# Group-norm statistics of the later batches through a DRAM round trip instead of two matrix products, in an attention kernel on one core

## The chip, the core and the metric

The kernel runs on one NeuronCore of a Trainium2 chip. The metric is the device time in microseconds (us) of one execution. Five engines work side by side, each through its own instructions in order: TensorE (PE in the profile, its weight loads PEld), VectorE (DVE), ScalarE (ACT), GpSimd (POOL) and SyncE (SP, here a queue for DMAs). They meet through semaphores.

## What is computed

The reference takes x of 32 images x 256 channels x 32 x 32 positions in float32, normalises it in groups of 8 channels, runs masked attention with 8 heads of 32 channels over the 1024 positions, and adds the result to x:

```python
def _gn(v, G=32, eps=1e-5):
    g = v.reshape(B_, G, C_ // G, H_, W_)
    m = jnp.mean(g, axis=(2, 3, 4), keepdims=True)
    s = jnp.var(g, axis=(2, 3, 4), keepdims=True)
    return ((g - m) / jnp.sqrt(s + eps)).reshape(v.shape)
# attention on _gn(x)
q = einsum('oc,bcs->bos', q_w, xf) + q_b     # likewise k and v from kv_w, kv_b
scores = einsum('bhqd,bhkd->bhqk', q, k) / sqrt(dk)
attn = softmax(where(mask == 0, -10000.0, scores)) with masked entries 0
out = einsum('bhqk,bhkd->bhqd', attn, v)
x = x + out
```

The mask keeps keys strictly before the query.

## The kernel before, in words

The function `unshifted` holds the whole fast path; `shifted` is a fallback that runs only when sums leave a range. Channels lie on the 128 partitions, in two halves g (NG = 2). A batch is one image. Its attention is cut into 12 visits: 6 per half g, each one entry of VISITS (line 583) with a long and a short block of scores for four heads. The loop over i at the end of `unshifted` runs 384 visits plus one. In each turn it emits `scores` of visit i, what is due `at` i, `values` of visit i - 1, what is due `between`, `add_keys` of visit i - 1, and what is due `after`. All five engines keep the order in which the code emits (`manual_schedule`, line 660), so these lists are an order written out by hand.

`scores(b, v)` (line 348) makes three PSUM tiles sT: two for the long block (heads 0 and 1, heads 2 and 3), one for the short block. The pool ps_s holds three such tiles, so each visit overwrites those of the visit before. In turn come the short products of heads 2 and 3, the long ones of heads 0 and 1, the long ones of heads 2 and 3, a wait of TensorE for the semaphore bank_free, and the short products of heads 0 and 1. Where a visit has two long entries and is in PAIRS (line 592), the second long entry of heads 0 and 1 is put between the two short products of heads 2 and 3, whose order is then turned round. A product is written by line L311 of the profile. ScalarE then takes the exponentials of the two long tiles (L397, written to e) and of the short one (L393, written to eh). For visits in PAIRS GpSimd masks eh into a diagonal tile with two selects (L339).

`values` (line 412) multiplies the exponentials with v into acc (L422). `add_keys` (line 434) sums exponentials on VectorE for the softmax denominators (L440): after visit 3's values comes one sum of 2048 elements per partition, after visit 4's first the sum e + diagonal, then e + e. `fold` and `stack` (lines 449 and 455) bring those sums together across partitions, by accumulating DMAs from GpSimd's queue and by SyncE's DMAs into folded; `finish` (line 539) multiplies, adds bias and residual on VectorE (L544, L547) and stores through SyncE.

One projection of the next batch (q, k or v, L169, from the normalised xn) is emitted in each visit, so the statistics of batch b are made while batch b - 1 is in its visits. `prepare(b, whens)` (line 637) lays them out with PREPARE (line 652), counted in visits from the first visit of b:

- `norm_channels`, once per half: two bn_stats (L184) and one bn_aggr (L185) on VectorE give each channel's mean and variance in mv.
- `norm_mean`: TensorE multiplies the means with avg (four products into pm, L169), ScalarE negates the result (L195).
- `norm_deviation`: three small VectorE instructions (L205 to L207).
- `norm_variance`: four products into pv, ScalarE adds eps (L219).
- `norm_rstd` (line 221): GpSimd raises to the power -0.5 (L227), then multiplies mean and rstd to shift (L229).
- `norm_apply` (line 231): ScalarE writes xn (L244). The first application stands in the after-list of the batch's visit 5, ahead of visit 6's exponentials on ScalarE.

For batches 2 to 31, pm comes after visit 3's scores and the values of visit 2, pv one visit later. Batch 0 is prepared ahead of the loop with its own forms of these steps, batch 1 in the first visits of batch 0. ALIGN (line 658) puts 24 drains on VectorE and 64 waits on GpSimd at the start.

Of the kernel before, what the change touches and what calls it, by code (L numbers as in the profile page):

```python
# [9 lines left out]
F32 = mybir.dt.float32  # L10
I32 = mybir.dt.int32
AF = mybir.ActivationFunctionType
ALU = mybir.AluOpType
# [4 lines left out]
P = 128  # L18
HD = 32
CPG = 8  # L20
HALF = 512
# [11 lines left out]
def tile_norm_attention_residual(  # L33
# [19 lines left out]
    nc = tc.nc  # L53
    B, C, H, W = x.shape
    S = H * W
    NG = C // P
    NB = S // P
    NH = S // HALF
# [3 lines left out]
    const = ctx.enter_context(tc.tile_pool(name="const", bufs=1))  # L62
# [26 lines left out]
    in_range = const.tile([P, ROW], F32, name="in_range")  # L89
    nc.gpsimd.memset(in_range, 1.0)  # L90
    inv_last = const.tile([P, 4, HALF // HD], F32, name="inv_last")
    eps = const.tile([P, 1], F32, name="eps")
    nc.gpsimd.memset(eps, 1e-5)

# [4 lines left out]
    def unshifted():  # L99
        live = {}  # L100
# [78 lines left out]
        def norm_channels(b, g):  # L179
            if g == 0:  # L180
                live["mv", b] = small.tile([P, NG, 2], F32, tag="mv", name=f"mv_{b}")
            st = small.tile([P, NH, 6], F32, tag="st", name=f"st_{b}_{g}")
            for c in range(NH):
                nc.vector.bn_stats(st[:, c, :], live["x", b][:, g, c * HALF : (c + 1) * HALF])  # L184
            nc.vector.bn_aggr(live["mv", b][:, g, :], st)  # L185

        def norm_mean(b):
            mv = live["mv", b]
            pm = misc(f"pm_{b}")
            product(pm[:, :NG], avg, mv[:, :, 0])  # L190
            if b == 0:
                live["dev", b] = small.tile([P, NG], F32, tag="dev", name=f"dev_{b}")
                nc.vector.tensor_sub(live["dev", b], mv[:, :, 0], pm[:, :NG])
            mean = small.tile([P, NG], F32, tag="mean", name=f"mean_{b}")
            nc.scalar.activation(mean, pm[:, :NG], AF.Identity, scale=-1.0)  # L195
            live["minus_mean", b] = mean

        def norm_deviation(b):
            mv, minus_mean = live["mv", b], live["minus_mean", b]

            if b == 0:
                dev = live["dev", b]
            else:
                dev = small.tile([P, NG], F32, tag="dev", name=f"dev_{b}")
                nc.vector.tensor_add(dev, mv[:, :, 0], minus_mean)  # L205
            nc.vector.tensor_mul(dev, dev, dev)
            nc.vector.tensor_add(dev, dev, mv[:, :, 1])  # L207
            live["dev", b] = dev

        def norm_variance(b):  # L210
            pv = misc(f"pv_{b}")
            product(pv[:, :NG], avg, live.pop(("dev", b)))
            rstd = small.tile([P, NG], F32, tag="rstd", name=f"rstd_{b}")
            live["rstd", b] = rstd
            if b == 0:

                nc.vector.tensor_scalar_add(rstd, pv[:, :NG], 1e-5)
                return
            nc.scalar.activation(rstd, pv[:, :NG], AF.Identity, bias=eps)  # L219

        def norm_rstd(b):
            rstd = live["rstd", b]
            if b == 0:

                nc.gpsimd.tensor_tensor(rstd, rstd, power, ALU.pow)
                return
            nc.gpsimd.tensor_tensor(rstd, rstd, power, ALU.pow)  # L227
            live["shift", b] = small.tile([P, NG], F32, tag="shift", name=f"shift_{b}")
            nc.gpsimd.tensor_tensor(live["shift", b], live["minus_mean", b], rstd, ALU.mult)  # L229

# [76 lines left out]
        def score(b, g, bank, j, op):  # L307

            c, kb, first, width, cols = op
            rows = slice(HD * j, HD * (j + 1))  # L310
            return nc.tensor.matmul(  # L311
                bank[c : c + KEYS, cols], lhsT=live["k", b, g][rows, kb * P + c : kb * P + c + KEYS],
                rhs=live["q", b, g][rows, first : first + width], start=True, stop=True, skip_group_check=True,
            )

        def scores_of(b, g, bank_of, heads, entries, between=lambda: None, order=slice(None)):
# [9 lines left out]
                                done.setdefault((j, c), []).append(score(b, g, bank_of(j), j, ops[n]))  # L326
            return done

        def mask(b, g, raw, j):


            hf, place = j // 2, (2 * j % 4) * P
            if ("e", b, g, "D", hf) not in live:
                live["e", b, g, "D", hf] = epool.tile(
                    [P, 4, HALF], F32, tag=("e0", "e")[hf], bufs=4, name=f"diagonal_{b}_{g}_{hf}"
                )
            square = live["e", b, g, "D", hf]
            for s in range(2):
                nc.gpsimd.affine_select(  # L339
                    out=square[:, :, place + s * P : place + (s + 1) * P],  # L340
                    in_=raw[:, :, (1 - s) * KEYS : (3 - s) * KEYS],
                    pattern=[[0, 4], [(1, -1)[s], P]], compare_op=ALU.is_gt, fill=0.0, base=0,
                    channel_multiplier=(-1, 1)[s],
                )
            if j == 0:
                nc.gpsimd.memset(square[0:1, :, 0:1], 1.0)

        def scores(b, v):
# [12 lines left out]
            long_of = lambda heads, n: scores_of(b, g, lambda j: pairs[j // 2][:, j % 2, :], heads, longs[n : n + 1])  # L361
            rest = [lambda: long_of((2, 3), 1)] if len(longs) > 1 else []
            begin = [lambda n=n: long_of((0, 1), n) for n in range(len(longs) - 1, -1, -1)]
            if i in PAIRS and len(longs) > 1:
                first = short_of((2, 3), begin.pop(0), slice(None, None, -1))
            else:
                first = short_of((2, 3))
# [222 lines left out]
        ]  # L590
        N, TOTAL = NG * len(VISITS), 2
        PAIRS = {0: 0, 1: 1, 3: 3, 4: 2}

        PRODUCTS = [
            (0, [
# [33 lines left out]
            10: [(("L", 4, Q(0, 4)), Q(0, 4)), (("D", 1, Q(0, 4)), Q(0, 4))],  # L629
            11: [(("L", 5, Q(0, 3)), Q(1, 4)), (("L", 5, Q(3, 4)), Q(3, 4)), (("H", 5, Q(0, 2)), Q(2, 4))],  # L630
        }
        at, between, after = {}, {}, {}

        def when(i, f, where=at):
            where.setdefault(i, []).append(f)

        def prepare(b, whens):
            for n, f in zip(whens, [
                lambda: norm_channels(b, 0), lambda: norm_channels(b, 1), lambda: norm_mean(b),
                lambda: norm_deviation(b), lambda: norm_variance(b), lambda: norm_rstd(b),  # L640
            ] + [lambda hf=hf, g=g: norm_apply(b, hf, g) for hf in range(NH) for g in range(NG)]):
                if n is None:
                    f()
                elif isinstance(n, tuple):
                    when(n[0], f, between)
                else:
                    when(n, f, after)

        PROJECT = (-5, -4, -3, -2, -1, 0, 1, 2, 3, 4, 5, 6)
        PREPARE = (-12, -11, -9, -9, -8, -8, -7, -6, -5, -3)
        SUMS = (3, 7, 10, 13)
        LOAD = 7
        SPREAD = (2, 2, 4, 5)
        FINISH = (N + 13, N + 13, N + 14, N + 16)
        every = range(4)
        ALIGN = 24, 64

        with tc.manual_schedule(engines={ENG.PE, ENG.Activation, ENG.DVE, ENG.Pool, ENG.SP}):  # L660

# [20 lines left out]
            if B > 1:  # L682
                nc.scalar.sem_inc(live["arrived"], 1)
                nc.sync.wait_ge(live["arrived"], 2)
                load(1)
            norm_deviation(0)
            norm_variance(0)
            turn_weights(0)
# [13 lines left out]
                else:  # L702
                    when(n, f)
            if B > 1:
                prepare(1, (None, None, 0, 1, 2, 2, 3, 4, 5, 7))
            for b in range(B):
                first, last = b * N, b == B - 1
                if b >= 1:
# [2 lines left out]
                if b >= 2:  # L711
                    for n in range(NG * NH):
                        cols = slice(n % NH * HALF, (n % NH + 1) * HALF)
                        v = max(first - 2 * N + LOAD, 0)
                        if n % NH == 0:
                            when(v, lambda n=n: with_scores(n // NH))
                        when(v, lambda b=b, n=n, cols=cols: load_part(b, n // NH, cols))
                    prepare(b, [(first + n,) if k in (2, 3) else first + n for k, n in enumerate(PREPARE)])
                if not last:
                    for n in every:  # L720
                        v = first + SUMS[n]
# [28 lines left out]
            for i in range(B * N + 1):  # L750
                if i < B * N:
                    scores(*divmod(i, N))
                for f in at.pop(i, ()):
                    f()
                b, v = divmod(i - 1, N)
                if i == B * N:

                    sums(3, SUMMED[v], False)
                if i:
                    values(b, v)  # L760
                    for f in between.pop(i, ()):
                        f()
# [7 lines left out]
            assert not at and not between and not after  # L770
            inside = end_last(B - 1)
        for p in reversed(pools):
            p.release()
# [171 lines left out]
```

## Time and profile before

| what | value |
|---|---|
| median of 3 runs | 1794.05 us (1794.01 to 1794.26) |
| the profiled execution's own time | 1793.44 us |
| its span, first to last instruction | 1791.7 us |
| granted TensorE clock | 0.999 |
| PE busy | 1784.4 us, 100% of the span |
| DVE busy | 1673.4 us, 93% |
| ACT busy | 1456.4 us, 81% |
| POOL busy | 881.3 us, 49% |
| from one batch's first score to the next one's | 55.09 us |

The page gives busy times by engine, the chain of work that ended last, and groups of instructions; a timeline gives a line for each run of equal instructions: start and length in us, engine, line of the kernel, operation, out<-in, shapes, count, and in brackets the idle time before it with what ended it. A float32 product is recorded as two passes, so four products appear as x8. Busy time of PE is modelled at its ends, so starts of successive runs are the better measure of what a step takes.

### The profile page before, as it was taken

The page shows a single profiled execution, that of the slowest core. Times are in us where ns is not written, and L with a number is a line of the kernel's source. Part 1 is how long each engine was busy: PE and PEld are TensorE (multiplying, and loading weights), DVE is VectorE, ACT ScalarE, POOL GpSimd, SP SyncE. Part 2 cuts the span into 40 slices and gives each one's busy share as a digit, 9 for nine tenths or more (in the row PEclk, how much of TensorE's full clock was granted, in tenths as well). Part 3 has the DMA queues.
Part 4 walks back from the last instruction along what each step waited for, and adds up shares of the span by engine and source line. Part 5 has one row for each costly group of instructions (what it writes and reads, how often), then busy time and mean ns, then how long its engine had stood idle before and what let it go on. Part 6 is the DMA issues. An engine that isn't in the chain of part 4 may idle for free.

```text
span 1791.7 us, 81825 instructions
## 1 busy us (share of the span) xinstructions
PE 1784.4 (100%) x37036; PEld 948.2 (53%) x37036; DVE 1673.4 (93%) x1826; ACT 1456.4 (81%) x1990; POOL 881.3 (49%) x903
## 2 busy tenths in 40 slices
PE   9999999999999999999999999999999999999998
PEld 5555555555555555555555555555555555555554
DVE  4689999999999999999999999999999999999998
ACT  6888878888788888788887888878888878888785
POOL 2345544554545555445554455454555544555452
PEclk9999999999999999999999999999999999999999
DMA  2566766767667766766676676767776667666664
GB/s 70 105 115 137 134 134 129 147 135 143 127 126 149 140 138 134 135 139 138 139 135 131 129 150 132 145 125 128 149 141 135 136 134 138 139 139 137 132 107 106
DMA packets 86818, 236.77 MB, mean 132 GB/s; under 512 B 21312, under 2 KB 22336, under 8 KB 70592
## 3 DMA queue, kind: packets, MB, share of 16 engines
q0 software_dynamic: 15872, 97.53, 40.1%
q1 hardware_dynamic: 70448, 133.89, 25.5%
q8 instruction: 290, 4.75, 1.1%
q14 instruction: 64, 0.52, 0.1%
q10 hardware_dynamic: 144, 0.07, 0.0%
HBM read 66.85 MB, written 34.57 MB: 57 GB/s over the span
## 4 chain that ended last, share of the span: by engine, by line
PE 99%; ACT 0%; DVE 0%; issue 0%; POOL 0%; POOLq 0%
PE sT L311 31%; PE acc L422 28%; PE pp L169 26%; PE ppv L169 13%; PE pd L474 1%; PE busy L155 0%; ACT e L397 0%; PE pv L169 0%; PE pm L169 0%; PE wt L148 0%; DVE rb_last L547 0%; ACT eh L393 0%; DVE rb_last L534 0%; DVE turned L531 0%; DVE acc L544 0%
## 5 line engine op out<-in xcount | busy, mean ns | idle before, releaser
L339 POOL TENSOR_SCALAR_AFFINE_SELECT diagonal<-eh 128x512 f32<-128x512 f32 x512 | 632.5, 1256 | 841.5 <-ACT eh L393 840.9
L397 ACT ACTIVATE e<-sT 128x1024 f32<-128x1024 f32 x768 | 744.4, 1022 | 250.3 <-PE sT L311 225.9
L440 DVE TENSOR_TENSOR e<-e,e 128x1024 f32<-128x1024 f32 x314 | 574.2, 1829 | 24.5 <-ACT v L275 3.2
L311 PE MATMUL sT<-q,k 32*64 32x128 f32 (+2 forms) x18432 | 578.4, 372 | 0.1
L311 PEld LDWEIGHTS sT<-q,k 32*64 32x64 f32 x18432 | 394.8, 131 | 188.4 <-PE sT L311 69.6
L169 PE MATMUL pp<-xn,wT 128*32 128x512 f32 x4096 | 492.2, 598 | 0.0
L422 PE MATMUL acc<-e,v 128*32 128x512 f32 (+3 forms) x4608 | 401.0, 450 | 0.0
L393 ACT ACTIVATE eh<-sT 128x768 f32<-128x768 f32 (+1 forms) x384 | 341.7, 890 | 0.0
L422 PEld LDWEIGHTS acc<-e,v 128*32 128x32 f32 x4608 | 149.2, 110 | 261.5 <-issue 238.9
L169 PE MATMUL ppv<-wT,xn 128*32 128x256 f32 x4096 | 247.5, 382 | 0.0
L440 DVE TENSOR_TENSOR diagonal<-diagonal,e 128x1536 f32<-128x1536 f32 x126 | 195.0, 1548 | 16.8 <-PE acc L422 9.2
L169 PEld LDWEIGHTS pp<-xn,wT 128*32 128x32 f32 x4096 | 107.0, 109 | 195.7 <-issue 163.7
L440 DVE TENSOR_TENSOR e<-e,eh 128x1024 f32<-128x1024 f32 x126 | 164.2, 1303 | 6.5
L422 PEld LDWEIGHTS acc<-diagonal,v 128*32 128x32 f32 x4096 | 121.1, 110 | 87.6 <-issue 76.0
L440 DVE TENSOR_TENSOR e<-e,diagonal 128x2048 f32<-128x2048 f32 x63 | 144.2, 2289 | 19.8 <-POOL diagonal L339 19.8
L169 PEld LDWEIGHTS ppv<-wT,xn 128*32 128x32 f32 x4096 | 120.1, 109 | 79.7 <-issue 7.0
L422 PE MATMUL acc<-diagonal,v 128*32 128x128 f32 x4096 | 158.7, 273 | 0.0
L244 ACT ACTIVATE xn<-x,shift,rstd 128x256 f32<-128x256 f32 x248 | 136.8, 608 | 0.6 <-POOL shift L229 0.6
L544 DVE TENSOR_TENSOR num<-num,rb 128x512 f32<-128x512 f32 x124 | 123.3, 994 | 0.2 <-DMA rb<-inverses 0.2
L453 POOL DMA_DIRECT2D e<-e x124 | 103.3, 833 | 38.2 <-issue 38.2
L547 DVE SCALAR_TENSOR_TENSOR rb<-num,v_bias_col,x 128x256 f32<-128x256 f32 x248 | 117.5, 515 | 4.4
L453 POOL DMA_DIRECT2D diagonal<-diagonal x124 | 104.1, 839 | 4.8 <-issue 4.8
(84 smaller groups left out, 984.4 us busy)
## 6 DMA issues: line engine op xcount, KB each, us to landing
x<-in_x_dram SPq DMA_DIRECT2D x124, 256.0 KB, 3.7
diagonal<-diagonal POOLq DMA_DIRECT2D x62, 512.0 KB, 5.4
e<-e POOLq DMA_DIRECT2D x62, 512.0 KB, 5.9
rb<-inverses SPq DMA_DIRECT2D x124, 256.0 KB, 3.9
out_dram<-rb SPq DMA_DIRECT2D x124, 256.0 KB, 4.9
diagonal<-diagonal POOLq DMA_DIRECT2D x62, 256.0 KB, 4.6
folded<-diagonal SPq DMA_DIRECT2D x62, 256.0 KB, 5.1
e<-e POOLq DMA_DIRECT2D x62, 256.0 KB, 5.0
```

What stands on the lines that cost most here:

```text
L169: nc.tensor.matmul(out[part], lhsT=lhsT[:, part], rhs=rhs, start=start, stop=stop, skip_group_check=True)
L244: nc.scalar.activation(to, of, AF.Identity, bias=live["shift", b][:, g : g + 1], scale=rstd)
L311: return nc.tensor.matmul(bank[c : c + KEYS, cols], lhsT=live["k", b, g][rows, kb * P + c : kb * P + c + KEYS], rhs=live["q", b, g][rows, ...
L339: nc.gpsimd.affine_select(out=square[:, :, place + s * P : place + (s + 1) * P], in_=raw[:, :, (1 - s) * KEYS : (3 - s) * KEYS], pattern=[ ...
L393: exp = nc.scalar.activation(eh.rearrange("p (n bank) q -> p bank n q", n=2)[:, :, :, :narrow], short[:, :, :, :narrow], AF.Exp)
L397: nc.scalar.activation(e[:, 2 * a : 2 * a + 2, :wide], pairs[a][:, :, :wide], AF.Exp)
L422: nc.tensor.matmul(acc[HD * j : HD * (j + 1), of], lhsT=live["v", b][:, kb, h * HD : (h + 1) * HD], rhs=e[:, j, :], start=first, stop=last ...
L440: nc.vector.tensor_add(to, to, tile_of(b, g, at))
L453: nc.gpsimd.dma_start(out=total[:rows], in_=total[rows : 2 * rows], accum_op=ALU.add)
L474: nc.tensor.matmul(pd[HD * j : HD * (j + 1), of], lhsT=pick, rhs=e[:, j, :], start=start, stop=stop, skip_group_check=True,)
L544: nc.vector.tensor_mul(num, num, rb)
L547: nc.vector.scalar_tensor_tensor(blocks(rb, s), blocks(num, s, (start + s) % 2 == 1), v_bias_col[:, g : g + 1], blocks(xt[:, g, cols], s), ...
```

## The change

For batches from 1 on, the group statistics no longer come from TensorE. All bn_stats results of a batch stay in one tile st (`norm_channels`, and bn_aggr is left to batch 0). `norm_gather` writes them to DRAM by a SyncE DMA. `norm_spread` reads them back by an indirect DMA on GpSimd's queue, so that each partition receives the statistics of all 8 channels of its group; the row to read is the partition's number shifted right by three, made once by an iota on GpSimd and a shift on VectorE. `norm_groups` aggregates them with two bn_aggr of 96 values each. `norm_signs` negates the mean and adds eps on GpSimd, where ScalarE did both. The statistics of the second half move ahead of that visit's `finish`, and `between` goes.

In `scores`, visits 3 and 4 of all batches but the last split the long product of heads 0 and 1 (512 queries) into 128 and 384; the 128 go between the short products of heads 2 and 3, whose order is turned round. In visits 2 and 8 of all batches but the last TensorE gets one more wait for a bank_free count, the one already waited for in `scores`. At the start VectorE has 84 drains instead of 24, GpSimd none of the 64 waits, SyncE 16 drains behind the load of batch 1. In the built order 77 of VectorE's 84 drains stand ahead of the shift that makes group_of, and 7 behind it.

```diff
         def norm_channels(b, g):
             if g == 0:
                 live["mv", b] = small.tile([P, NG, 2], F32, tag="mv", name=f"mv_{b}")
-            st = small.tile([P, NH, 6], F32, tag="st", name=f"st_{b}_{g}")
+                live["st", b] = small.tile([P, NG, NH * 6], F32, tag="st", bufs=1, name=f"st_{b}")
+            st = live["st", b][:, g, :].rearrange("p (c s) -> p c s", c=NH)
             for c in range(NH):
                 nc.vector.bn_stats(st[:, c, :], live["x", b][:, g, c * HALF : (c + 1) * HALF])
-            nc.vector.bn_aggr(live["mv", b][:, g, :], st)
+            if b == 0:
+                nc.vector.bn_aggr(live["mv", b][:, g, :], st)
+
+        def norm_gather(b):
+            n = NH * 6
+            each = live["each", b] = dram.tile([P, NG * n], F32, tag="st", name=f"each_{b}")
+            nc.sync.dma_start(out=each, in_=live.pop(("st", b)).rearrange("p g s -> p (g s)"))
+
+        def norm_spread(b):
+            n = NH * 6
+            eight = small.tile([P, HALF], F32, tag="turned", bufs=1, name=f"eight_{b}")[:, : CPG * NG * n]
+            live["eight", b] = eight.rearrange("p (c g s) -> p c g s", c=CPG, g=NG)
+            nc.gpsimd.indirect_dma_start(
+                eight, None, live["each", b].rearrange("(m c) s -> m (c s)", c=CPG),
+                bass.IndirectOffsetOnAxis(ap=group_of[:, 0:1], axis=0),
+            )
+
+        def norm_groups(b):
+            for g in range(NG):
+                nc.vector.bn_aggr(live["mv", b][:, g, :], live["eight", b][:, :, g, :])
+
+        def norm_signs(b):
+            mv = live["mv", b]
+            live["minus_mean", b] = small.tile([P, NG], F32, tag="mean", name=f"mean_{b}")
+            nc.gpsimd.tensor_scalar(live["minus_mean", b], mv[:, :, 0], -1.0, None, ALU.mult)
+            live["rstd", b] = small.tile([P, NG], F32, tag="rstd", name=f"rstd_{b}")
+            nc.gpsimd.tensor_scalar(live["rstd", b], mv[:, :, 1], 1e-5, None, ALU.add)
...
+        def part_of(b, g, bank, entry, of):
+            at, _, halves = entry
+            for j in (0, 1):
+                for ((c, kb, first, _, cols),) in halves:
+                    score(b, g, bank[:, j, :], j, (
+                        c, kb, first + of.start, of.stop - of.start, slice(cols.start + of.start, cols.start + of.stop)
+                    ))
...
+            if b < B - 1 and v in SPLIT:
+                begin = [lambda n=n: part_of(b, g, pairs[0], longs[0], n) for n in (slice(0, P), slice(P, HALF))]
-            if i in PAIRS and len(longs) > 1:
+            if i in PAIRS and len(begin) > 1:
...
-                lambda: norm_channels(b, 0), lambda: norm_channels(b, 1), lambda: norm_mean(b),
-                lambda: norm_deviation(b), lambda: norm_variance(b), lambda: norm_rstd(b),
+                lambda: norm_channels(b, 0), lambda: norm_channels(b, 1), lambda: norm_gather(b), lambda: norm_spread(b),
+                lambda: norm_groups(b), lambda: norm_signs(b), lambda: norm_rstd(b),
...
-        PREPARE = (-12, -11, -9, -9, -8, -8, -7, -6, -5, -3)
+        PREPARE = (-12, -11, -10, -10, -9, -8, -8, -7, -6, -5, -3)
-        ALIGN = 24, 64
+        EVEN = 2, 8
+        ALIGN = 84, 0, 16
...
-                prepare(1, (None, None, 0, 1, 2, 2, 3, 4, 5, 7))
+                prepare(1, (None, None, None, None, 1, 2, 2, 3, 4, 5, 7))
...
-                    prepare(b, [(first + n,) if k in (2, 3) else first + n for k, n in enumerate(PREPARE)])
+                    prepare(b, [
+                        (first + n, after) if k == 1 else first + n for k, n in enumerate(PREPARE)
+                    ])
...
+                    for _ in range(EVEN.count((i - 1) % N) if i < B * N - N else 0):
+                        nc.tensor.wait_ge(bank_free, live["free"])
```

More of the change, by code (lines that the diff above doesn't have):

```diff
@@ L91, in tile_norm_attention_residual @@
     inv_last = const.tile([P, 4, HALF // HD], F32, name="inv_last")
+    place = const.tile([P, 1], mybir.dt.uint32, name="place")
+    nc.gpsimd.iota(place, pattern=[[0, 1]], base=0, channel_multiplier=1)
+    group_of = const.tile([P, 1], mybir.dt.uint32, name="group_of")
+    nc.vector.tensor_scalar(group_of, place, 3, None, ALU.logical_shift_right)
     eps = const.tile([P, 1], F32, name="eps")
@@ L190, in norm_mean @@
             product(pm[:, :NG], avg, mv[:, :, 0])
-            if b == 0:
-                live["dev", b] = small.tile([P, NG], F32, tag="dev", name=f"dev_{b}")
-                nc.vector.tensor_sub(live["dev", b], mv[:, :, 0], pm[:, :NG])
+            live["dev", b] = small.tile([P, NG], F32, tag="dev", bufs=1, name=f"dev_{b}")
+            nc.vector.tensor_sub(live["dev", b], mv[:, :, 0], pm[:, :NG])
             mean = small.tile([P, NG], F32, tag="mean", name=f"mean_{b}")
@@ L198, in norm_deviation @@
         def norm_deviation(b):
[L199 to L205, printed above, removed]
+            mv, dev = live["mv", b], live["dev", b]
             nc.vector.tensor_mul(dev, dev, dev)
             nc.vector.tensor_add(dev, dev, mv[:, :, 1])
-            live["dev", b] = dev
         def norm_variance(b):
@@ L214, in norm_variance @@
             live["rstd", b] = rstd
[L215 to L219, printed above, removed]
+            nc.vector.tensor_scalar_add(rstd, pv[:, :NG], 1e-5)
         def norm_rstd(b):
             rstd = live["rstd", b]
+            nc.gpsimd.tensor_tensor(rstd, rstd, power, ALU.pow)
             if b == 0:
-                nc.gpsimd.tensor_tensor(rstd, rstd, power, ALU.pow)
                 return
-            nc.gpsimd.tensor_tensor(rstd, rstd, power, ALU.pow)
             live["shift", b] = small.tile([P, NG], F32, tag="shift", name=f"shift_{b}")
@@ L592, in unshifted @@
         PAIRS = {0: 0, 1: 1, 3: 3, 4: 2}
+        SPLIT = 3, 4
         PRODUCTS = [
@@ L631, in unshifted @@
         }
-        at, between, after = {}, {}, {}
+        at, after = {}, {}
         def when(i, f, where=at):
@@ L644, in prepare @@
                 elif isinstance(n, tuple):
-                    when(n[0], f, between)
+                    n[1].setdefault(n[0], []).insert(0, f)
                 else:
@@ L685, in unshifted @@
                 load(1)
+            for _ in range(ALIGN[2]):
+                nc.sync.drain()
             norm_deviation(0)
@@ L759, in unshifted @@
                 if i:
+                    for _ in range(EVEN.count((i - 1) % N) if i < B * N - N else 0):
+                        nc.tensor.wait_ge(bank_free, live["free"])
                     values(b, v)
-                    for f in between.pop(i, ()):
-                        f()
                     if b < B - 1 or v not in SUMMED or v == 1:
@@ L769, in unshifted @@
                     f()
-            assert not at and not between and not after
+            assert not at and not after
             inside = end_last(B - 1)
```

## The prediction

> **What bounds the kernel now.** I read the page's busy times and its chain first, then timelines of TensorE, GpSimd, VectorE and ScalarE over one steady batch (visits from 624.75 us to 679.84).
>
> ```profile
> PE 1784.4 (100%) x37036; PEld 948.2 (53%) x37036; DVE 1673.4 (93%) x1826; ACT 1456.4 (81%) x1990; POOL 881.3 (49%) x903
> ...
> PE 99%; ACT 0%; DVE 0%; issue 0%; POOL 0%; POOLq 0%
> ```
>
> TensorE is never out of work: the chain is 99% PE, and its score runs (L311) show that batches 1 to 31 start 55.09 us apart. So a PE instruction taken away counts in full, and so does any new wait. TensorE around the two products that go:
>
> ```profile
> 638.08 1.47 PE L311 MATMUL sT<-q,k 32*64 32x128 f32 x48
> ...
> 642.95 0.22 PE L169 MATMUL pm<-mv,avg 128*32 128x2 f32 x8
> 643.10 1.48 PE L311 MATMUL sT<-q,k 32*64 32x128 f32 x48
> ...
> 647.56 0.22 PE L169 MATMUL pv<-dev,avg 128*32 128x2 f32 x8
> 647.71 1.55 PE L311 MATMUL sT<-q,k 32*64 32x256 f32 x48
> ...
> 665.66 1.47 PE L311 MATMUL sT<-q,k 32*64 32x128 f32 x48
> ...
> 670.65 1.47 PE L311 MATMUL sT<-q,k 32*64 32x128 f32 x48
> ```
>
> Visits 3 and 9 do the same work, but 3 ends with pm: 5.025 us against 4.989.
>
> Next, who feeds TensorE. GpSimd, VectorE and ScalarE in that batch:
>
> ```profile
> 647.03 3.68 POOL L339 TENSOR_SCALAR_AFFINE_SELECT diagonal<-eh 128x512 f32<-128x512 f32 x2 [2.25 <-ACT eh L393]
> 650.68 1.15 POOL L227 TENSOR_TENSOR rstd<-rstd,power 128x2 f32<-128x2 f32 x1
> 651.91 0.31 POOL L229 TENSOR_TENSOR shift<-mean,rstd 128x2 f32<-128x2 f32 x1
> ```
> ```profile
> 645.22 1.23 DVE L440 TENSOR_TENSOR e<-e,e 128x1024 f32<-128x1024 f32 x1
> 646.36 1.22 DVE L440 TENSOR_TENSOR e<-e,eh 128x1024 f32<-128x1024 f32 x1
> 647.62 2.60 DVE L440 TENSOR_TENSOR e<-e,e 128x2048 f32<-128x2048 f32 x1
> 650.14 1.11 DVE L544 TENSOR_TENSOR num<-num,rb 128x512 f32<-128x512 f32 x1
> 651.29 0.88 DVE L547 SCALAR_TENSOR_TENSOR rb<-num,v_bias_col,x 128x256 f32<-128x256 f32 x2
> 652.09 2.29 DVE L440 TENSOR_TENSOR e<-e,diagonal 128x2048 f32<-128x2048 f32 x1
> ```
> ```profile
> 651.62 0.70 ACT L258 ACTIVATE q<-pp,qk_bias 128x512 f32<-128x512 f32 x1
> 652.26 1.10 ACT L244 ACTIVATE xn<-x,shift,rstd 128x256 f32<-128x256 f32 x2
> 653.52 1.94 ACT L397 ACTIVATE e<-sT 128x1024 f32<-128x1024 f32 x2 [0.17 <-PE sT L311]
> 655.35 0.82 ACT L393 ACTIVATE eh<-sT 128x768 f32<-128x768 f32 x1
> 656.04 0.70 ACT L258 ACTIVATE k<-pp,qk_bias 128x512 f32<-128x512 f32 x1
> ```
>
> The shift ends at 652.22, xn (L244) starts 0.03 later, and behind it on ScalarE stand the exponentials of visit 6, whose last (eh) must end before TensorE's visit 7 at 656.90 overwrites that bank. Read the GpSimd ends against the VectorE ends: the selects end at 650.71, 0.49 after the 2048-wide sum (650.22); the power at 651.83, 0.58 after L544 (651.25); the shift 0.05 after the second L547 (652.17). In all 31 batches shift ends 51 to 56 ns after the end of a two-input VectorE instruction.
>
> **The Trainium skill.** "SBUF — State Buffer", Who interferes with whom: a VectorE instruction with two SBUF inputs contends with a GpSimd instruction that reads SBUF; whichever holds the pair keeps it for its whole instruction. The ends above agree. "TensorEngine Tiling (Array Packing)", Key Properties: changing the tiling mode drains TensorE. That agrees with visit 9: the last product run ends with an extra 113 ns before the scores, which pm, itself 149 ns, hides. "DMA: Bandwidth & Descriptors", Anatomy of one DMA: about 2.0 us fixed per GpSimd-issued DMA; the trace shows 4.6 to 5.9 us for the kernel's large ones.
>
> **The change, part by part.**
>
> *pm and pv go* (batches 2 to 31): 5.025 - 4.989 = 0.036, and visit 4 against 10, 4.606 - 4.552 less 0.010 for a different projection = 0.044. Together 0.080 x 30 = 2.4 us. Batch 1's pair, in batch 0, gives 0.04 and 0.43 (pv there waits 0.39 for ScalarE's k, then nets 0.04).
>
> *The split*: in visit 3 heads 0 and 1 start 53 ns after heads 2 and 3, behind eight weight loads; in visit 0, which interleaves as the new form does, 27 ns, yet its phase is 1.419 against 1.403. So each split phase costs between -0.022 and +0.016; I take -0.022: 2 x 31 x 0.022 = 1.4 us, and -1.0 at the other end. EVEN's waits name a count already reached; TensorE's queue is ahead by whole products (PEld idles on "issue" 0.3 us at a time), so nothing; without that lead 62 waits at 0.04 (a satisfied wait on GpSimd) would be 2.5 us.
>
> *Start*: 77 of the 84 drains at 39.6 ns (spacing of the 24 now) end at 3.88, the shift of the iota 0.16 (as L217), 7 more drains: VectorE starts at 4.33 instead of 3.56, but the fourth x part lands only at 6.26, so the second bn_aggr ends at 7.51 instead of 7.20. pm waited to 7.61 for avg, held by GpSimd's 64 waits; they go, so pm starts near 7.57. Zero; if x landed sooner, up to the 0.77 of VectorE would show. SyncE's 16 drains (0.6 us at that spacing) end near 10.4, before the first gather's data at 14.2. Zero, and still short of visit 1, which reads the result, if that data came at once.
>
> *VectorE and ScalarE*: per batch two 0.21 and three 0.16 instructions go from VectorE, two aggregates of 96 values come. Price: 0.21 (12 values) plus 84 at bn_stats' 0.69/512 = 0.32 at least; if all of 0.21 over a 0.16 small instruction is per value, 0.6. I take 0.3. ScalarE loses 0.17 and 0.26, idle there anyway.
>
> *The gather on SyncE* stands behind folded (635.91, 0.51) and ahead of the output DMAs (644.77): issue at 636.5. `inverses`, issued as closely behind folded, lands with it; folded takes 5.1, so about 641.0. *The spread* holds GpSimd from the earlier DMA issue (done 635.7) to then: nothing is queued but visit 3's select, at 642.0. Not in the trace: the indirect issue (L453's is 0.83) and its flight (2.0 by the skill to 5.0): landing 644 to 647. Behind the waiting aggregates on VectorE stand the sums.
>
> *Signs and eps on GpSimd* decide. Walk the new order. VectorE's sum into diagonal waits for TensorE's visit-2 products, so it starts at 638.17, not 639.39: statistics now stand earlier. Adding trace durations, the two 1024-wide sums end at 645.91 (were 647.58); aggregates to 646.35; the 2048-wide sum runs 646.27 to 648.56, before visit 4's first select can ask (eh ends 646.87). Then GpSimd gets one turn per VectorE end: first select 649.06, L544 649.60; second select 650.09, first L547 650.37; sign 650.42, second L547 650.77; eps 650.82. The 2048-wide e+diagonal has begun at 650.69 and ends 652.98: power 653.56. The next 2048-wide sum, 653.09 to 655.38, holds the shift: 655.43. Before, power and shift took the turns that sign and eps have now. xn at 655.47, its two 1.10, exponentials 2.65 to the end of eh, 0.06 to TensorE: visit 7 at 659.28 instead of 656.90. That is 2.38 per batch and swallows the 0.080 and the split, which lie before it. 30 x 2.38 = 71.3.
>
> **Sum.** The profiled execution's own time is 1793.44 (span 1791.7 and 1.7 around it); 1793.44 + 71.3 - 0.5 (batch 0) = 1864.2. The runs' median lies 0.6 above: **1865**.
>
> **Rivals.** *A turn earlier*: if the aggregates end after 647.05 (0.6 each, or landing after 646.5), the first select goes ahead of the 2048-wide sum, power gets the second L547's end, and the shift ends with e+diagonal, 653.97 to 654.4. Visit 7 is 0.9 to 1.3 late: 26 to 38 us, about 1825. For it: both unknown prices reach there. Against: each only at its upper end.
>
> *All four fit* (the other side): GpSimd's chain ends by 652.9, since visit 7, by then 0.12 earlier, allows xn 3.81 before 656.78. It needs VectorE to be idle once before e+diagonal, or tiny GpSimd instructions to slip in two to a turn. Then the gains stand: 2.4 + 0.5 + 1.4 = 4.3, 1789.1, in the median 1789.8. For it: shift has 0.7 us to spare, and ScalarE and VectorE lose work. Against: 31 of 31 shifts waited out a VectorE end, and four turns do not fit where two just did. With the split at its bad end the gain is 1.9: no change.
>
> *A late landing*: beyond 648 the shift follows the landing by some 6.6 us; 1890 and more.
>
> **Chances.** Late shift by two long sums (forecast) 0.37, a turn earlier 0.17, late landing 0.03: slower 0.57. All fit: 0.33 faster, 0.03 with the bad split the same; gains cancelled by something small, 0.07: same 0.10. I take 0.2% as about what a measurement of this kernel can tell from no change. The forecast's own range, from the price of the aggregates and the turn earlier, is 1817 to 1882; for eight in ten the range must reach the fitting case: 1788.5 to 1882.
>
> **What would show it.** Right: per batch a TensorE gap before visit 7, its releaser ScalarE's eh; ScalarE's xn waiting on GpSimd's shift; sign, eps, power and shift each ending 0.05 or 0.58 after a VectorE sum. Gone pm and pv should still shorten visits 3 and 4 by 0.04 each, and split phases should read 1.38 or 1.42. Wrong: shift near 652.5 with VectorE idle before e+diagonal, or an aggregate far over 0.6.

## The result, and the profile after

The kernel after takes 1822.84 us (median of 6 runs, 1821.08 to 1827.05) against 1794.03 for the kernel before (6 runs beside it): a ratio of 1.016, 95% interval 1.0147 to 1.0173. The profiled execution has a span of 1821.0 us (before 1791.7), at a granted clock of 0.999 in both. The direction is the forecast's, the size is not: 71 us were forecast, 28.8 came.

Below, "at 22.8" means 22.8 us after the first score of the batch; "the port" is the pair of SBUF ports that the prediction has VectorE and GpSimd contend for, and a "turn" is the end of a VectorE instruction at which a waiting GpSimd instruction gets through. Batch 11 after starts at 636.45 us. The profiled spans differ by 29.3 us, and the starts of the visits say where. The first score comes 0.40 later. Batch 0 is 0.71 shorter. Batch 1 is 4.83 longer. Batches 2 to 30 are 24.6 longer together: 23 of them by 0.59 to 0.67 each, six (8, 9, 17, 19, 25, 27) by 1.0 to 2.4. The end adds 0.12. The six are those in which the gather landed latest: the spread's issue begins at 17.8 to 18.5 in them, at 17.7 or sooner in the 23.

The page's busy times and its chain of work that ended last, after:

```profile
PE 1807.2 (99%) x37036; PEld 934.0 (51%) x37036; DVE 1656.3 (91%) x1734; ACT 1433.6 (79%) x1928; POOL 922.3 (51%) x997
...
PE 91%; DMA 3%; POOL 3%; issue 2%; ACT 1%; DVE 1%; DVEq 0%; ACTq 0%
```

TensorE has the same number of instructions, by chance (the split adds as many as go), and is "busy" 22.8 us longer, because the ends of its products are modelled and a product that waits counts as busy. The chain is the better sign: 99% PE before, 91% now, with GpSimd, DMA and ScalarE in it. That DMA stands in it with 3% is no proof that the round trip costs them: experiment 1 keeps both DMAs and loses nothing. VectorE and ScalarE have less work than before; that bought nothing.

GpSimd after, in batch 1 (no `finish` there yet) and in batch 11:

```profile
98.21 2.32 POOL L217 TENSOR_SCALAR mean<-mv 128x2 f32<-128x2 f32 x1
100.59 2.33 POOL L219 TENSOR_SCALAR rstd<-mv 128x2 f32<-128x2 f32 x1
103.00 2.29 POOL L245 TENSOR_TENSOR rstd<-rstd,power 128x2 f32<-128x2 f32 x1
...
653.81 1.17 POOL L205 DMA_INDIRECT eight<-each,group_of  x1 [6.41 <-DMA each<-st]
654.98 2.37 POOL L368 TENSOR_SCALAR_AFFINE_SELECT diagonal<-eh 128x512 f32<-128x512 f32 x2
...
658.65 3.35 POOL L368 TENSOR_SCALAR_AFFINE_SELECT diagonal<-eh 128x512 f32<-128x512 f32 x2 [0.49 <-ACT eh L424]
662.09 0.54 POOL L217 TENSOR_SCALAR mean<-mv 128x2 f32<-128x2 f32 x1
662.70 0.45 POOL L219 TENSOR_SCALAR rstd<-mv 128x2 f32<-128x2 f32 x1
663.23 0.82 POOL L245 TENSOR_TENSOR rstd<-rstd,power 128x2 f32<-128x2 f32 x1
664.13 1.59 POOL L249 TENSOR_TENSOR shift<-mean,rstd 128x2 f32<-128x2 f32 x1
```

An instruction on 128 x 2 numbers takes 0.45 to 2.33 us, since its time is that of the VectorE instruction it waits out; in batch 1 only long sums are there to wait for, and three of the four cost 2.3 each. VectorE in batch 11, from the sums into diagonal on, then ScalarE:

```profile
650.31 3.08 DVE L471 TENSOR_TENSOR diagonal<-diagonal,e 128x1536 f32<-128x1536 f32 x2
...
655.27 1.58 DVE L471 TENSOR_TENSOR e<-e,e 128x1024 f32<-128x1024 f32 x1
656.78 1.65 DVE L471 TENSOR_TENSOR e<-e,eh 128x1024 f32<-128x1024 f32 x1
658.35 1.02 DVE L212 BATCH_NORM_AGGREGATE mv<-eight 128x2 f32<-128x96 f32 x2
659.29 2.22 DVE L471 TENSOR_TENSOR e<-e,e 128x2048 f32<-128x2048 f32 x1
661.44 1.11 DVE L575 TENSOR_TENSOR num<-num,rb 128x512 f32<-128x512 f32 x1
662.58 0.88 DVE L578 SCALAR_TENSOR_TENSOR rb<-num,v_bias_col,x 128x256 f32<-128x256 f32 x2
663.38 2.28 DVE L471 TENSOR_TENSOR e<-e,diagonal 128x2048 f32<-128x2048 f32 x1
```
```profile
665.75 1.10 ACT L264 ACTIVATE xn<-x,shift,rstd 128x256 f32<-128x256 f32 x2 [1.85 <-POOL shift L249]
666.76 1.91 ACT L428 ACTIVATE e<-sT 128x1024 f32<-128x1024 f32 x2
668.57 0.80 ACT L424 ACTIVATE eh<-sT 128x768 f32<-128x768 f32 x1
```

The sign ends 0.1 after L575, eps 0.08 after the first L578 (663.06), the power 0.59 after the second (663.46), and the shift at 665.72, 0.06 after the sum e+diagonal (665.66). That is the forecast's order of turns with one long sum fewer: this is the rival "a turn earlier". ScalarE stands idle for 1.85 us before xn, and eh of visit 6 ends at 32.92 instead of 31.42.

TensorE then loses time, but at another place than forecast. The scores of visit 7, before and after, and what follows them after:

```profile
656.90 1.47 PE L311 MATMUL sT<-q,k 32*64 32x128 f32 x48
...
668.49 2.02 PE L331 MATMUL sT<-q,k 32*64 32x128 f32 x48
670.43 2.09 PE L173 MATMUL pp<-xn,wT 128*32 128x512 f32 x16
```

Visit 7's scores begin at 32.04, on time, 0.88 before eh ends; the run takes 2.02 where it took 1.47 before. Within it the long products of heads 0 and 1 start 0.05 after the second exponential of visit 6 ends, those of heads 2 and 3 start at 32.97, 0.05 after eh ends. Visit 7 needs the three banks of visit 6 one after the other: only its last third waits for eh. It lasts 5.26 us instead of 4.56.

### The profile page after: what moved, and what is told of

It reads as the page before. It is cut to its first block, busy times and chain, and to the rows that moved or that the text cites. A ratio compares the mean times of both kernels' runs of the same rounds, so it can differ in the third digit from the quotient of the medians.

```text
span 1821.0 us, 81846 instructions
## 1 busy us (share of the span) xinstructions
PE 1807.2 (99%) x37036; PEld 934.0 (51%) x37036; DVE 1656.3 (91%) x1734; ACT 1433.6 (79%) x1928; POOL 922.3 (51%) x997
## 4 chain that ended last, share of the span: by engine, by line
PE 91%; DMA 3%; POOL 3%; issue 2%; ACT 1%; DVE 1%; DVEq 0%; ACTq 0%
PE sT L331 28%; PE acc L453 25%; PE pp L173 25%; PE ppv L173 12%; DMA each<-st 2%; DMA eight<-each,group_of 1%; ACT e L428 1%; POOL mean L217 1%; POOL diagonal L368 1%; POOL shift L249 1%; PE pd L505 1%; DVE st L189 0%; POOL rstd L245 0%; POOL rstd L219 0%; ACT xn L264 0%
## 5 line engine op out<-in xcount | busy, mean ns | idle before, releaser
L368 POOL TENSOR_SCALAR_AFFINE_SELECT diagonal<-eh 128x512 f32<-128x512 f32 x512 | 541.2, 1080 | 612.0 <-ACT eh L424 611.9
L331 PE MATMUL sT<-q,k 32*64 32x64 f32 (+1 forms) x18928 | 597.7, 367 | 6.5 <-ACT e L428 6.2
L471 DVE TENSOR_TENSOR e<-e,e 128x1024 f32<-128x1024 f32 x314 | 565.0, 1799 | 24.1 <-ACT v L295 4.0
L173 PE MATMUL pp<-xn,wT 128*32 128x512 f32 x4096 | 497.8, 600 | 0.0
L471 DVE TENSOR_TENSOR diagonal<-diagonal,e 128x1536 f32<-128x1536 f32 x126 | 188.7, 1498 | 16.3 <-issue 5.9
L471 DVE TENSOR_TENSOR e<-e,eh 128x1024 f32<-128x1024 f32 x126 | 194.1, 1541 | 6.5
L205 POOL DMA_INDIRECT eight<-each,group_of x31 | 42.3, 1364 | 199.0 <-DMA each<-st 199.0
L578 DVE SCALAR_TENSOR_TENSOR rb<-num,v_bias_col,x 128x256 f32<-128x256 f32 x248 | 119.1, 521 | 4.4
```

The lines of the kernel that those rows point to most:

```text
L173: nc.tensor.matmul(out[part], lhsT=lhsT[:, part], rhs=rhs, start=start, stop=stop, skip_group_check=True)
L205: nc.gpsimd.indirect_dma_start(eight, None, live["each", b].rearrange("(m c) s -> m (c s)", c=CPG), bass.IndirectOffsetOnAxis(ap=group_of[ ...
L331: return nc.tensor.matmul(bank[c : c + KEYS, cols], lhsT=live["k", b, g][rows, kb * P + c : kb * P + c + KEYS], rhs=live["q", b, g][rows, ...
L368: nc.gpsimd.affine_select(out=square[:, :, place + s * P : place + (s + 1) * P], in_=raw[:, :, (1 - s) * KEYS : (3 - s) * KEYS], pattern=[ ...
L471: nc.vector.tensor_add(to, to, tile_of(b, g, at))
L578: nc.vector.scalar_tensor_tensor(blocks(rb, s), blocks(num, s, (start + s) % 2 == 1), v_bias_col[:, g : g + 1], blocks(xt[:, g, cols], s), ...
```

## Experiments

All times are medians; each ratio is to the kernel before, run beside it. In most of these kernels sign and eps are on ScalarE, behind the aggregates, which leaves power and shift on GpSimd as before the change: "two on GpSimd".

**1. Sign and eps back on ScalarE.**

```diff
-            nc.gpsimd.tensor_scalar(live["minus_mean", b], mv[:, :, 0], -1.0, None, ALU.mult)
+            nc.scalar.activation(live["minus_mean", b], mv[:, :, 0], AF.Identity, scale=-1.0)
...
-            nc.gpsimd.tensor_scalar(live["rstd", b], mv[:, :, 1], 1e-5, None, ALU.add)
+            nc.scalar.activation(live["rstd", b], mv[:, :, 1], AF.Identity, bias=eps)
```

> Kernel after, with sign and eps on ScalarE: two small GpSimd instructions (power, shift) are left in the chain, as before the change. Theory (each small GpSimd instruction takes one end of a VectorE instruction): power takes the end of L575, shift that of the first or second L578, so shift ends 26.6 to 27.1 us after the batch's first score, earlier than before (27.46); TensorE does not wait in visit 7 and batch 1's two long visits are gone. 1793.4 + 0.4 (start) - 0.7 (batch 0) - 30 x 0.11 = 1789.8, between 1788.5 and 1791.5. Rival (the round trip is the cost: the spread that holds GpSimd, later selects, the aggregates): nothing of that changes, so 1815 or more.

Measured: 1790.64 us, 0.998 (0.9972 to 0.9988). Every batch from 1 to 30 takes 54.98; before it was 55.09. Shift ends at 26.4 to 27.3, at 26.43 in batch 11 (from 623.34):

```profile
649.57 0.19 POOL L249 TENSOR_TENSOR shift<-mean,rstd 128x2 f32<-128x2 f32 x1
```

The whole loss of the change goes with these two instructions, batch 1's included, and the gain of what the change took from TensorE is left. The round trip through DRAM, which this kernel keeps, is not the cost by itself: the batches with late statistics here (shift at 27.3) are as short as the others.

**2. The same two turns in the kernel before.** Two instructions that change nothing, ahead of the power:

```diff
+            nc.gpsimd.tensor_scalar(live["minus_mean", b], live["minus_mean", b], 1.0, None, ALU.mult)
+            nc.gpsimd.tensor_scalar(rstd, rstd, 0.0, None, ALU.add)
             nc.gpsimd.tensor_tensor(rstd, rstd, power, ALU.pow)
```

> Kernel before, with two small GpSimd instructions ahead of the power (the negated mean times one, the variance plus zero, in place); no DRAM round trip, no split. Theory: they take the ends of L544 and the first L547, power takes the second L547's, shift ends with e+diagonal at 29.7 instead of 27.47 after the batch's first score; TensorE waits in visit 7 by 0.7 to 1.2 a batch: 1794 + 30 x (0.7 to 1.2) + up to 5 in batch 1 = 1815 to 1835. Rival (the round trip is the cost): 1794 to 1796.

Measured: 1826.81 us, 1.0182 (1.0166 to 1.0197). Visit 7 takes 5.55 in most batches. GpSimd in batch 11 (from 637.63), which ends the shift at 29.68, forecast 29.7:

```profile
664.48 0.75 POOL L229 TENSOR_TENSOR rstd<-rstd,power 128x2 f32<-128x2 f32 x1
665.31 1.99 POOL L231 TENSOR_TENSOR shift<-mean,rstd 128x2 f32<-128x2 f32 x1
```

Two tiny instructions, with no DRAM, no gather and no split, cost as much as the whole change. They alone suffice. The turns were not quite the expected ones: the second addition took 0.21 us and no turn of its own, and the power ends 0.59 after the first L547, not the second. By then e+diagonal had begun, so shift ends with it all the same; the 29.7 owes something to luck.

**3. Three and five instead of four.** Three: only the sign goes to ScalarE. Five: one more addition of zero on GpSimd.

> Kernel after, with only the sign on ScalarE: three small GpSimd instructions. Theory: eps takes the end that the sign took (L575, at 26.1), power takes that of the first L578 (26.62) and ends near 27.2; e+diagonal has begun by then (26.94), so shift still ends with it at 29.28, as with four instructions: 1820 to 1824, nothing won by taking one away. Rival (each instruction costs its share): half of the way back, 1805 to 1808. Rival (round trip): 1822.

> Kernel after, with a fifth small GpSimd instruction in the chain (it adds zero to the variance that eps was added to). Theory: the fifth takes the second L578's end, power waits out e+diagonal (29.2), shift the next 2048-wide sum: it ends near 31.55, 2.3 later. The turn that the forecast had charged is thereby paid: each of three banks of visit 7 comes free 2.28 later, the last costs TensorE 2.3 more per batch, 30 x 2.3 = 69: about 1890, 1875 to 1900. Rival (round trip, with small instructions at their own 0.23 us): 1822 to 1830.

Measured: three, 1798.06 (1.0024, 1.0017 to 1.0031; single runs from 1792.5 to 1805.3); five, 1860.81 (1.0371, 1.0324 to 1.0418). Both expectations fail. Three instructions win 24.8 of the 28.8 us back, where nothing was expected and half by the rival; five stay 14 us under their range. Two batches of the kernel with three, a long one and an ordinary one (they start at 404.22 and 625.23), show why:

```profile
426.43 3.27 POOL L368 TENSOR_SCALAR_AFFINE_SELECT diagonal<-eh 128x512 f32<-128x512 f32 x2 [1.76 <-ACT eh L424]
429.68 0.65 POOL L219 TENSOR_SCALAR rstd<-mv 128x2 f32<-128x2 f32 x1
431.43 1.99 POOL L249 TENSOR_TENSOR shift<-mean,rstd 128x2 f32<-128x2 f32 x1
...
647.43 1.22 POOL L368 TENSOR_SCALAR_AFFINE_SELECT diagonal<-eh 128x512 f32<-128x512 f32 x2 [0.49 <-ACT eh L424]
648.64 2.25 POOL L219 TENSOR_SCALAR rstd<-mv 128x2 f32<-128x2 f32 x1
652.07 0.30 POOL L249 TENSOR_TENSOR shift<-mean,rstd 128x2 f32<-128x2 f32 x1
```

At 22.8 two instructions ask for the port almost at once: the second select of visit 4 and the 2048-wide sum behind the aggregates. In the first batch the sum starts at 22.73, before the select (22.80), which then takes 2.68; shift ends at 29.19 and visit 7 takes 5.18. In the second the sum starts at 22.86, the select is through in 0.63 and the sum waits for it; every later turn comes one VectorE instruction earlier, shift ends at 27.14 and visit 7 takes 4.56. A few ns can decide this, and the recorded starts are not quite the order of the requests. In 14 batches of the kernel after, the sum starts 0.046 to 0.053 us after the select by the record and still goes first (batch 11 above is one: its second select starts at 659.24, the sum at 659.29); in seven it starts 0.056 to 0.059 after, and the select goes first. In the profiled execution of three only batches 7 and 24 fell the first way, the two in which the gather landed first (16.88, against 16.97 or later); its time was 1792.5, the lowest of all, and each such batch adds 0.62, so the other executions fit some nine more of them, though no trace shows these. With four instructions both ways end at 29.3. With five, the select first still ends at 29.35, and the sum first at 31.6 to 32.1, the long sum more that I had foreseen for every batch: the eight batches of this kind are 2.3 to 5.4 us longer than the ordinary 55.76. In batch 7 the sum goes ahead of both selects, shift ends at 33.69 and the batch is 6.1 longer.

**4. Is it that race?** In the kernel with three, one aggregate shorter, which leaves out seven of eight channels of one half's statistics, or one aggregate made twice.

```diff
-                nc.vector.bn_aggr(live["mv", b][:, g, :], live["eight", b][:, :, g, :])
+                nc.vector.bn_aggr(live["mv", b][:, g, :], live["eight", b][:, :1 if g else CPG, g, :])
```
```diff
-            for g in range(NG):
+            for g in (0, 1, 1):
                 nc.vector.bn_aggr(live["mv", b][:, g, :], live["eight", b][:, :, g, :])
```

> The kernel with three small GpSimd instructions, in which the second aggregate takes 12 values instead of 96 (one channel stands for its group of eight in that half: part of the statistics is left out), so 0.21 us instead of 0.52. Theory of the port race: with three instructions a batch stalls or not by who takes the shared port at 22.8 us, the second select of visit 4 (free in 0.63, no stall) or the 2048-wide sum behind the aggregates (then the select takes 2.7 and the stall is 0.62). Less work on VectorE lets the sum win in every batch: 1792.5 + 27 x 0.62 = 1809, between 1804 and 1813, slower for less work. Rival (aggregates cost by their length): 1792 or less, always faster than the 1798 with long ones.

> The kernel with three small GpSimd instructions, in which the second aggregate is made twice. Theory of the port race: the sum now comes 0.45 later than the second select in every batch, so none stalls: 1791.5, between 1790 and 1793.5, and a narrow spread over executions; faster for more work. Rival (aggregates cost by their length): 1798 or more.

Measured: shorter, 1806.59 (1.0074, 1.006 to 1.0088); made twice, 1792.80 (0.9993, 0.9985 to 1.0002). Less work on VectorE makes the kernel 8.5 us slower than the 1798.06, more work makes it 5.3 faster. In the shorter one the sum starts at 22.48 and the select waits it out in 22 of the 29 batches from 2 on (in six of the other seven the statistics landed late); in the other the select goes first in all 29. The race is shown.

**5. The smaller parts.** Without split and additional waits, and each of the two left out by itself, all with two on GpSimd:

```diff
-        SPLIT = 3, 4
+        SPLIT = ()
-        EVEN = 2, 8
+        EVEN = ()
```

> The kernel with two small GpSimd instructions (sign and eps on ScalarE), without the split of visits 3 and 4 and without the additional waits in visits 2 and 8. From one batch to the next 54.98 with them; without, by the theory that a split phase saves 0.015 to 0.022 and a wait nothing, 55.01 to 55.02: 1.0 to 1.3 us in all, so 1791.7. Rival (the split saves nothing or costs): 54.98 or less, 1790.6 or less.

> The kernel with two small GpSimd instructions (sign and eps on ScalarE) once more, unchanged, beside the three that follow on one chip: 1790.6 within 1, batches of 54.98. If it comes out above 1793, the differences of the other three to their expected times are the chip's and not theirs.

> The kernel with two small GpSimd instructions, without the additional waits of TensorE in visits 2 and 8, with the split. The waits name a count already reached; by the prediction they cost nothing, so 1790.6 and batches of 54.98, no stalls. Rival (they hold TensorE's stream of instructions in a place that keeps it from standing still within runs of products, as it did in ten visits of the kernel without split and waits, 4 us in all): 1793 to 1795.

> The kernel with two small GpSimd instructions, without the split, with the additional waits. From the batches of the kernel without both (55.010) and with both (54.979): the split saves 0.031 a batch, 0.97 in all, so batches of 55.01 and 1791.6. Rival (the split, not the waits, keeps TensorE from standing still within runs): 1795.

Measured: neither, 1796.02 (1.001, 1.0002 to 1.0019); both, once more, 1789.97 (0.9981, 0.9973 to 0.9988); without the waits, 1790.13 (0.9981, 0.9973 to 0.9989); without the split, 1798.31 (1.0024, 1.0017 to 1.0031). So with the split the waits cost and bring nothing. Without it the kernel that has them is the slower by 2.3 us, but the two intervals overlap, so for whole products that stays open. The split saves 0.031 to 0.035 a batch in the undisturbed visits (54.98 against 55.01), some 1 us. Yet the kernels with whole products are 6 to 8 us slower than with the split, and both expectations for them fail: in single visits (1 and 10 above all, seven to eleven batches in a profile) TensorE stands still inside a run of products for 0.1 to 1.5 us, with no semaphore named. That the split keeps TensorE from this, the rival of the last expectation, agrees with the times; how it would, no run shows. The longest has a line among TensorE's waits, in the kernel that lacks only the split:

```profile
PE sT L331 <- issue: 1.2, 1, 1.2
```

With the split, the profiles of experiments 5 and 6 have one to three longer batches each, by 0.60 at most. The larger of these, but for one of 0.43 in visit 10, have another cause, late statistics: in batch 19 of the repeated kernel ScalarE idles 2.48 us for the aggregates with the sign at the head of its order, and visit 6 takes 0.40 more. So the round trip can cost with two on GpSimd too, if little.

The kernel before has whole products too and does not stand still. What brings it on stays open. The page also shows a DMA queue for instructions (q8, 290 packets before); whether these come late in such places, no run tests.

**6. The start.** 24 drains on VectorE instead of 84, with none or with the change's 16 on SyncE.

```diff
-        ALIGN = 84, 0, 16
+        ALIGN = 24, 0, 16
```

> The kernel with two small GpSimd instructions, with the drains of before at the start (24 on VectorE, none on SyncE) and still without GpSimd's 64 waits. Theory: the later first score (16.40 against 16.00) comes from VectorE's 84 drains; without them the second aggregate ends near 7.2, the product of the means starts near 7.35 since avg is ready, and the first score comes near 15.7: 1789.9. Rival (the x parts landed 0.3 later by chance): first score stays at 16.3 to 16.4.

> The kernel with two small GpSimd instructions, with 24 drains on VectorE and the change's 16 on SyncE. First score at 15.68 as with 24 and none. If the 2.2 us between the last output DMA's issue and the end, which that kernel had more than the others, go with SyncE's drains, they are gone here: 1789.9, the fastest of all. If they go with VectorE's drains: 1792.1.

Measured: none on SyncE, 1792.61 (0.9993, 0.9984 to 1.0001); 16 on SyncE, **1789.71** (0.9979, 0.997 to 0.9987), faster than both kernels of the study and the lowest median here, though not clear of the 1789.97 of experiment 5. The first score comes at 15.68 and 15.78 instead of 16.40: VectorE's drains were what made the start late. Without SyncE's drains the profiled execution has 2.2 us more between its last output DMA's issue and its end, so that 1789.9 was missed; with them that is gone. The trace puts it on SyncE: 2.65 us between two of its closing semaphore instructions, where the kernel with the 16 drains has 0.06. Yet the kernel before has none of these drains and no such pause either, so they do not decide it alone. Why, no run shows.

## Why the prediction was wrong in size

**Right.** The mechanism: TensorE bounds, sign and eps take turns at the port, shift becomes late, xn waits for it, eh is late for visit 7. "SBUF — State Buffer", Who interferes with whom (the Trainium skill) says that the shared port pair is an exclusive lock and that issue order decides who blocks; the batches of experiment 3 agree, with 0.63 or 2.68 us for the same select. pm and pv: 55.091 against 55.011 with whole products is 0.080 a batch, forecast 0.080. The waits: nothing. The split: 0.016 to 0.018 a phase, forecast 0.022. Batch 0: 0.71 shorter, 0.2 more than forecast.

**The step that failed** is the order of instructions at visit 4: "aggregates to 646.35; the 2048-wide sum runs 646.27 to 648.56, before visit 4's first select can ask". The sum was to start at 21.52 and starts at 22.85, behind the first select (22.20). With one select ahead of the sum GpSimd needs one turn fewer, and shift ends with e+diagonal, at 29.27 instead of 30.68. Three terms of the walk were too small, by 1.33 together:

- 0.44: the sums into diagonal start at 13.86, not 13.42. TensorE does not hold them then, as the forecast had it; VectorE comes straight from a finish that ran late, since it had idled 0.76 for TensorE's acc ahead of the second bn_stats.
- 0.38: from there to the end of the 1024-wide sums it takes 8.12, not 7.74. I let the spread hold GpSimd until the data land, but they land at 17.4 (forecast 16.3) and its issue takes 1.33 in the median (forecast 0.83), so it is done at 18.5, while eh of visit 3 had been ready since 17.2. "Nothing is queued but visit 3's select" was true, and those selects then run beside the 1024-wide sums, which take 1.58 and 1.65 instead of 1.23 and 1.22.
- 0.51: the aggregates keep VectorE 0.87, not 0.36 (0.52 and 0.58 each instead of 0.3).

The margin was 0.68 (22.20 less 21.52). By these lengths no term alone breaks the order and any two do; that is worked out from the trace, no run takes them out one by one. Two observations fit. In batch 7 of experiment 1 the data land at 16.32, as forecast, and the selects start at 17.43: the stretch takes 7.64, but begins at 14.50, and the sum still comes behind the select. With the short aggregate of experiment 4 the sum starts at 22.48, still behind the first select (22.20).

**The price of a late shift** was too high too. In all batches from 2 to 30 of the kernel after and of experiment 2, the batch is longer than 55.09 by the end of shift less 28.68, to within 0.01: 0.59 at 29.27, 1.0 at 29.68, 2.01 at 30.69. The forecast's price also grows one for one, but from 28.30 on, since I had all of visit 7 wait for eh, and it waits for three banks in turn. So before the change shift had 1.2 us to spare, not 0.7. In batch 17 a late landing put shift where the forecast had it: 2.01 instead of 2.38. Of the 2.38, then, 1.41 was the order and 0.38 the price; 0.59 is left.

**The rival "a turn earlier"** (0.17, about 1825) is what came. Its condition, aggregates that end after 22.3, is met (22.92), though not by its two ways, aggregates of 0.6 or a landing after 21.7: slips on three terms did it. Its price of 0.9 to 1.3 a batch was too high; batch 1 and the six dear batches made up for that, so its nearness to 1822.84 is partly luck.

**Left out of the sum.** Batch 1 was one of 30 equal batches, but there no short VectorE instruction offers an end, and it costs 4.83. A late landing was given 1890 and more for the whole kernel; it comes in single batches: in 17, 19 and 25 the indirect DMA takes 5.6 to 5.7 us instead of 3.0, the aggregates end near 25, and the batch is 2.0 to 2.4 longer. The start: 0 forecast, 0.40 measured. VectorE's 77 drains ended at 4.4, not at 3.88, with pauses of 0.46 and 0.18 among them that the 24 of before did not show.

Together: 23 batches at 0.62, six dearer ones with 10.3, batch 1 with 4.8, the start 0.4, less 0.7 in batch 0: 29.1 of the 29.3.

## What to carry to other kernels

A tiny GpSimd instruction that reads SBUF beside a VectorE full of two-input sums can cost the rest of whatever sum it meets (up to 2.3 us here), not its own 0.2 us; put small scalar steps on ScalarE, or count VectorE's ends before adding one. On ScalarE they then wait for the statistics ahead of the exponentials, which cost 0.4 us in a late batch here. Where such a chain has just enough turns, 0.1 us of VectorE work or less decides who gets the port, and the kernel's time then jumps by several us in the unexpected direction; a wide spread over equal executions can be a sign of it. For a late exponential, ask which bank each later product needs, since a visit can begin long before the last one is free; and fit the cost against the end of the late step over single batches, which gives the slack of the path to 0.01 us here.

## What the runs showed of the hardware that was not expected

- bn_aggr of 96 values takes 0.52 to 0.59 us; of 12 values 0.21, or 0.15 right behind another (experiment 4).
- Of a GpSimd select and a VectorE sum that ask for the port together, some ns of the recorded starts tell who goes first: the sum up to 0.053 us after the select's start, the select from 0.056 on (kernel after).
- The indirect DMA's issue holds GpSimd for 1.1 to 2.2 us (1.33 in the median) beyond its wait for the data; the data land 3.0 us after its start in the median, at most 5.7.
- A small GpSimd instruction can slip in free: in experiment 2 the second addition took 0.21, by the record within the first L547, which is no longer than elsewhere (0.48).
- TensorE standing still within product runs when the split is left out (experiment 5), and SyncE 2.65 us between two semaphore instructions at the end of the kernel without its drains (experiment 6): both measured, neither explained.
